# Eight single PSUM banks in one ring in place of one four-bank tile and four single banks

## The chip, the core and the metric

The kernel runs on one core of a Trainium2 chip. TensorE (PE) multiplies and writes its results to PSUM, an accumulator memory of eight banks; one bank holds 512 float32 columns on 128 partitions. VectorE (DVE) and ScalarE (ACT) read PSUM; GpSimd (POOL) does small elementwise work and starts indirect transfers; SyncE (SP) starts the other transfers. The metric is the device time of one execution in microseconds (us). A change counts as faster or slower by its time against the kernel before.

## The reference: what is computed

Two transformer layers over x of shape (8, 256, 128), in float32. Each layer is attention, then a mixture of eight experts, with a layer norm ahead of each and a residual around each:

```python
x = x + _L0_attn_ref(_layernorm(x), ...)   # causal softmax attention, 16 heads of 8, rope, 4 key-value heads
x = x + _L0_ffn_ref(_layernorm(x), ...)    # top-2 of 8 experts, 128 -> 512 -> 128, gelu, plus a shared expert
x = x + _L1_attn_ref(_layernorm(x), ...)   # linear attention in segments of 32, with gated retrieval of past states
x = x + _L1_ffn_ref(_layernorm(x), ...)    # top-2 of 8 experts, 128 -> 512 -> 128, relu
```

In the first attention, with `scale = D ** -0.5`:

```python
scores = jnp.einsum('bqhd,bkhd->bhqk', q, k) * scale
scores = jnp.where(causal[None, None], -jnp.inf, scores)
w = jax.nn.softmax(scores, axis=-1)
out = jnp.einsum('bhqk,bkhd->bqhd', w, v).reshape(b, s, E)
return out @ Wout + bout
```

In the second attention the part that matters here is, for each segment, `A = einsum('bnchk,bndhk->bnhcd', pqc, pkc) * tri`, its product with the values, and a sum over the states of earlier segments weighted by gates.

## The kernel before

The 2048 rows of x stay in SBUF as four batches `xs[b]` of four tiles of 128 rows; a sequence ("row" in the code, class `Row`, L524) is two tiles. There are eight such rows, two to a batch.

**PSUM.** Two pools share the eight banks (L92, L93). `quad()` (L104) gives the one tile `sc` of four banks, for anything that needs four 512-column results at once; `bank()` (L101) gives one of four single banks `mm`. There is one `sc` tile, so whoever wants it next waits until its last reader is done.

**First attention** (`attention0`, L671). For each row, `maxima` (L598) makes the score groups with queries on the partitions and takes their negated maxima; `weighted` (L620) makes them again with keys on the partitions, takes the exponential and multiplies by the values. A score group (`scores`, L580) is four matmuls of 32 rows each (L586), one for each key-value head `j` on the partitions `32j` to `32j+32`, and each writes one bank. Where the tile lies on the diagonal, four more matmuls (L592) add a causal mask of bfloat16, with an identity as weights. Per row there are three groups in `maxima` and three in `weighted`, two of each three masked. One DVE instruction reads all four banks (L608), or one ACT instruction (L637). L640 multiplies by the values into a single bank, DVE copies it out (L648), L651 turns it, L657 and L659 divide, and L663 transposes each half into `oT_bank`, which is held from the start of `weighted`; after the second half `project` (L503) copies and multiplies by the output weights. `maxima` of row r+1 alternates with `weighted` of row r; the preparation of row r+2 (L251, L537 to L576) comes ahead of them. After each second row, `route0` (L690) chooses experts, with a layer norm, `logits` (L301) and small DVE steps.

**Second attention** (`attention1`, L734), by batch. L748 makes four projections of 512 columns, one for each tile, in one `sc` tile; ACT scales the first 256 columns (L752) and the next 128 (L756) of each, DVE copies the last 128 of all four (L761). Then, for each pair of tiles, POOL makes `vm` (L822), PE makes the states (L835, L841, L849), and for each tile k there are four scores of 32 rows (L877), one DVE product with `tri` over the four banks (L881), 16 small matmuls with the values (L891), a copy on ACT (L897), L905, the division (L911 to L914) and a transpose (L917). After `project`, four matmuls (L938) give the states' part, DVE multiplies by the gates, two heads at a time (L946), and sums (L952). The product and POOL's `vm` share one buffer, tagged `vm`.

**Experts** (`experts`, L400): rows are gathered in slots, L431 multiplies by the first weights, ACT or DVE applies the function, L446 multiplies by the second. `dispatch` (L318) finds the slots and sends rows to them by indirect transfers (L368); `chosen` (L475) fetches results the same way (L480).

**Order.** Python generators are woven together: the first attention with the experts of half 0, then the second attention of each batch with the experts of the other half (`weave`, L1007 and L1027 to L1035). A scheduler then fixes one instruction order for each engine by priority and by the buffers that are free; each engine runs its own order strictly and waits on semaphores. `follow(j)` (L108) raises the priority of the matmuls after the first of a group, so that those of a group stand next to each other.

Of the kernel before, what the change touches and what calls it, by code (L numbers as in the profile page):

```python
# [39 lines left out]
P = 128  # L40
B, S, D = 8, 256, 128
NBLK = 4
NT = 4
# [34 lines left out]
def two_layers(  # L78
# [12 lines left out]
    dram = ctx.enter_context(tc.tile_pool(name="slots", bufs=1, space=bass.MemoryType.DRAM))  # L91
    ps4 = ctx.enter_context(tc.tile_pool(name="ps4", bufs=1, space=PSUM))  # L92
    ps1 = ctx.enter_context(tc.tile_pool(name="ps1", bufs=4, space=PSUM))  # L93

    names = iter(range(10**6))

    def tl(pool, shape, tag, dt=FP, bufs=None):
        kw = {} if bufs is None else {"bufs": bufs}
        return pool.tile(shape, dt, tag=tag, name=f"{tag}_{next(names)}", **kw)

    def bank():  # L101
        return tl(ps1, [P, 512], "mm")

    def quad():  # L104

        return tl(ps4, [P, G, 512], "sc")

# [155 lines left out]

    def small(tag, shape=(P, NT, E)):
        return tl(sm, list(shape), tag)

# [51 lines left out]
    def dispatch(half, b1s):  # L318
# [17 lines left out]

        c3, tiles = small("cap3", (P, E, HT)), small("tiles", (P, E))
        nc.vector.tensor_tensor(
            c3, last(pc[:, 0:E], HT), const("cap").rearrange("p (e c) -> p e c", e=E), ALU.is_gt
        )  # L340
        nc.vector.tensor_reduce(tiles, c3, AX.X, ALU.add)
        u3, ends, starts = small("upto3", (P, E, E)), small("ends", (P, E)), small("starts", (P, E))
        nc.vector.tensor_tensor(
# [5 lines left out]

        base, pos = small("base", (P, E)), small("pos", (P, HT, E))  # L350
# [4 lines left out]
        ph, at = small("posk", (P, 2, HT, E)), small("at", (P, 2, HT))  # L355
        nc.vector.tensor_tensor(
# [167 lines left out]
    class Row:  # L524
# [55 lines left out]
        def scores(self, lhsT, rhs, mask):  # L580

            sc = quad()
            for j in range(KVH):
                rows = slice(32 * j, 32 * j + 32)
                with follow(j):
                    nc.tensor.matmul(  # L586
                        sc[:, j, :], lhsT=lhsT[rows], rhs=rhs[rows], start=True, stop=mask is None
                    )
            for j in range(KVH):
                if mask is not None:  # L590
                    with follow(1):
                        nc.tensor.matmul(  # L592
                            sc[:, j, :].rearrange("p (i k) -> p i k", i=G), lhsT=identb, rhs=mask,
                            start=False, stop=True,
                        )
            return sc

        def maxima(self):  # L598

            for qt in range(2):  # L600
                nms = []
                for kt in range(qt + 1):
                    nm = small(f"nmax{kt}", (P, KVH, G))
# [4 lines left out]
                    nc.vector.tensor_reduce(  # L608
                        nm, sc.rearrange("p j (i k) -> p j i k", i=G), AX.X, ALU.max, negate=True
                    )  # L610
                    nms.append(nm)
                    if kt == qt:
                        dst = self.qx[:, qt, :, :, HD].rearrange("p i j -> p j i")
                        if qt:
                            nc.vector.tensor_tensor(dst, *nms, ALU.min)
                        else:
                            nc.vector.tensor_copy(dst, nms[0])
                    yield

        def weighted(self):  # L620
            oT_bank = bank()
            for qt in range(2):
# [9 lines left out]
                for kt in range(qt + 1):  # L632
                    sc = self.scores(
                        self.kxT[:, kt * P : (kt + 1) * P], qm, causTb if kt == qt else None
                    )
                    pT = tl(big, [P, KVH, BT], "at", bufs=2)
                    nc.scalar.activation(pT, sc, AF.Exp)  # L637
                    for j in range(KVH):
                        with follow(j):
                            nc.tensor.matmul(  # L640
                                po[32 * j : 32 * j + 32, :], lhsT=self.vx[:, kt, j, :],
                                rhs=pT[:, j, :], start=(kt == 0), stop=(kt == qt),
                            )
                    if kt < qt:
                        yield
# [4 lines left out]
                for i in range(G):  # L650
# [11 lines left out]
                )  # L662
                nc.tensor.transpose(  # L663
                    oT_bank[:, qt * P : (qt + 1) * P], on.rearrange("p j i d -> p (j i d)"), ident
                )
# [68 lines left out]
    def attention1(x):  # L734
# [12 lines left out]
        for t in range(NT):  # L747
            nc.tensor.matmul(  # L748
                pp[:, t, :], lhsT=xlT[:, t * P : (t + 1) * P], rhs=wqkvu, start=True, stop=True
            )  # L750
        for t in range(NT):
            nc.scalar.activation(  # L752
                s2[:, t].rearrange("p a d -> p (a d)"), pp[:, t, 0 : 2 * D],
                AF.Copy, scale=r[:, t : t + 1],
            )
            nc.scalar.activation(  # L756
                va1[:, t, :, 0:HD],
                pp[:, t, 2 * D : 3 * D].rearrange("p (h c) -> p h c", h=H),
                AF.Copy, scale=r[:, t : t + 1],
            )  # L760
        nc.vector.tensor_copy(u, pp[:, :, 3 * D :])  # L761

# [54 lines left out]
        for b in range(RB):  # L817
# [49 lines left out]

            oT_bank = bank()
            for k in range(2):
# [4 lines left out]
                for j in range(G):  # L874
                    rows = slice(32 * j, 32 * j + 32)
                    with follow(j):
                        nc.tensor.matmul(  # L877
                            sc[:, j, :].rearrange("p (i k) -> p i k", i=G),
                            lhsT=pkT[rows, cols], rhs=pqm[rows, :, cols], start=True, stop=True,
                        )  # L880
                nc.vector.tensor_tensor(  # L881
                    at.rearrange("p j i k -> p (j i) k"),
                    sc.rearrange("p j (i k) -> p (j i) k", i=G),
                    const("tri").unsqueeze(1).to_broadcast([P, H, P]), ALU.mult,
                )

# [17 lines left out]
                for i in range(G):  # L904
# [7 lines left out]
                nc.vector.reciprocal(rec, rec)  # L912
                on = tl(wk, [P, G, G, HD], "on")
# [3 lines left out]
                nc.tensor.transpose(  # L917
                    oT_bank[:, k * P : (k + 1) * P], on.rearrange("p j i d -> p (j i d)"), ident
                )
                yield  # L920
            pw = project(oT_bank, wot_s)
            xo = tl(wk, [P, 2, D], "xo", bufs=1)
            nc.vector.tensor_tensor(xo, pw, xl[:, t0 : t0 + 2, :], ALU.add)

            for k in range(2):
# [9 lines left out]
                for j in range(G):  # L935
                    rows = slice(32 * j, 32 * j + 32)
                    with follow(j):
                        nc.tensor.matmul(  # L938
                            py[:, j, 0 : n_seen * 32].rearrange("p (n i c) -> p n i c", i=G, c=HD),
                            lhsT=pqT[rows, t * P : (t + 1) * P], rhs=st4[rows, 0:n_seen, :, 0:HD],  # L940
                            start=True, stop=True,
                        )
# [177 lines left out]
```

## Time and profile before

| | |
|---|---|
| median of 3 runs | 1099.59 us (1095.2 to 1102.19) |
| profiled execution, its own time | 1101.3 us |
| its span, first to last instruction | 1099.5 us |
| mean granted TensorE clock | 0.697 |
| busy: PE, DVE, ACT, POOL | 655.6, 423.0, 243.8, 211.5 us |
| chain that ended last, by engine | PE 48%, DVE 18%, POOL 10%, ACT 9%, issue 8%, DMA 5% |

The page lists groups of instructions by line: engine, operation, output from input with their shapes, how many, then busy us and mean ns of one, then how long the engine was idle just before them and what ended that idle time. A line of the timeline has the start in us, the length in us, the engine, the line of the code, and in brackets the idle time before it with its cause. A line of the table of stretches has its bounds, then length, busy us and count of PE, of its weight loads (PEld), of DVE, ACT and POOL, then the granted clock (1 is full), the share of DMA time and GB/s. Matmuls in float32 appear as two passes each.

### The profile page before, as it was taken

The numbers are of one execution on the slowest core, as the hardware profiler recorded it, in microseconds if no ns is written. First come the engines' busy times: TensorE is split into PE (matmuls) and PEld (weight loads), VectorE is DVE, ScalarE is ACT, GpSimd is POOL, SyncE is SP. The second block draws the span as 40 slices with busy tenths as digits, with TensorE's granted clock in tenths as the row PEclk, the third lists the DMA queues.
The fourth block names the chain that finished last, engine by engine and source line by source line (L and its number), as shares of the span: only waits on it lengthen the run. The fifth ranks groups of instructions, "written<-read, shape, count | busy, mean of one in ns | idle before, by whom it ended". The sixth has DMA issues, their size and how long they took to land.

```text
span 1099.5 us, 11701 instructions
## 1 busy us (share of the span) xinstructions
PE 655.6 (60%) x4154; PEld 444.6 (40%) x4170; DVE 423.0 (38%) x1121; ACT 243.8 (22%) x505; POOL 211.5 (19%) x267
## 2 busy tenths in 40 slices
PE   3666555655566677775138649873059759730970
PEld 2222221324122454465115427773037647630970
DVE  4422433235131513041246545442247657541431
ACT  1212121201213434431121014341022122200320
POOL 5000100003300000006440220104721120166005
PEclk9856557655565868876665559995559869955995
DMA  7000000001200222314400004743204413214861
GB/s 213 1 0 1 0 1 1 1 1 52 82 0 20 77 58 58 89 53 129 133 14 1 1 0 129 206 117 112 62 6 135 125 46 87 66 48 134 261 207 55
DMA packets 103786, 76.35 MB, mean 69 GB/s; under 512 B 7520, under 2 KB 89776, under 8 KB 103728
## 3 DMA queue, kind: packets, MB, share of 16 engines
q1 hardware_dynamic: 98304, 66.04, 20.8%
q0 software_dynamic: 4096, 8.40, 2.4%
q10 hardware_dynamic: 1328, 1.17, 0.4%
q8 instruction: 33, 0.54, 0.2%
q14 instruction: 25, 0.20, 0.1%
HBM read 61.30 MB, written 14.29 MB: 69 GB/s over the span
## 4 chain that ended last, share of the span: by engine, by line
PE 48%; DVE 18%; POOL 10%; ACT 9%; issue 8%; DMA 5%; another core or an unknown queue 1%; SPq 0%; POOLq 0%; ACTq 0%; DVEq 0%
PE sc L586 7%; PE mm L431 7%; PE mm L446 6%; DVE nmax L608 5%; POOL yt L480 4%; ACT at L637 4%; PE sc L592 3%; PE mm L640 3%; POOL xg L368 3%; PE sc L748 2%; PE sc L877 2%; PE mm L891 2%; DMA w<-in_w 2%; PE mm L497 2%; PE mm L905 1%
## 5 line engine op out<-in xcount | busy, mean ns | idle before, releaser
L441 ACT ACTIVATE hT<-mm,bias 128x128 f32<-128x128 f32 x276 | 84.9, 371 | 234.9 <-PE mm L431 198.1
L446 PE MATMUL mm<-w,hT 128*128 128x128 f32 x736 | 114.1, 295 | 18.4 <-issue 11.8
L431 PE MATMUL mm<-xrT,w 128*128 128x128 f32 x736 | 117.1, 314 | 6.9 <-DVE xrT L415 6.0
L431 PEld LDWEIGHTS mm<-xrT,w 128*128 128x128 f32 x736 | 106.3, 224 | 17.9 <-DVE xrT L415 10.4
L446 PEld LDWEIGHTS mm<-w,hT 128*128 128x128 f32 x736 | 100.8, 206 | 26.0 <-issue 13.7
L608 DVE TENSOR_REDUCE nmax<-sc 128x16 f32<-128x2048 f32 x24 | 55.0, 2291 | 109.4 <-PE sc L586 71.7
L480 POOL DMA_INDIRECT yt<-yg,slots x64 | 62.3, 974 | 102.9 <-DMA yg<-ys 58.9
L368 POOL DMA_INDIRECT xg<-hrows,slots x64 | 66.6, 1040 | 79.1 <-DVE slots L361 60.8
L640 PE MATMUL mm<-at,vx 128*32 128x512 f32 x192 | 37.7, 871 | 48.9 <-ACT at L637 48.9
L637 ACT ACTIVATE at<-sc 128x2048 f32<-128x2048 f32 x24 | 45.1, 1877 | 81.7 <-PE sc L592 69.7
L586 PE MATMUL sc<-qm,kxT 32*128 32x512 f32 x192 | 42.6, 970 | 25.5 <-DVE nmax L608 16.6
L223 POOL TENSOR_SCALAR rsqrt<-mv 128x4 f32<-128x4 f32 (+1 forms) x24 | 6.1, 254 | 256.2 <-DVE mv L233 251.1
L648 DVE COPY os<-mm 128x512 f32<-128x512 f32 x16 | 11.1, 691 | 113.4 <-PE mm L640 102.0
L251 PE MATMUL mm<-ident,xl 128*128 128x128 f32 x16 | 4.1, 404 | 80.9 <-DVE xl L240 80.9
L955 POOL TENSOR_TENSOR x<-x,hr 128x128 f32<-128x128 f32 x16 | 7.4, 465 | 229.8 <-DVE x L928 216.2
L439 DVE TENSOR_SCALAR hT<-mm,bias 128x128 f32<-128x128 f32 x92 | 31.4, 348 | 36.5 <-ACT hT L441 36.2
L586 PE MATMUL sc<-km,qT 32*128 32x512 f32 x192 | 43.0, 982 | 1.7 <-DVE nmax L608 1.7
L881 DVE TENSOR_TENSOR at<-sc,consts 128x2048 f32<-128x2048 f32 x16 | 36.6, 2287 | 13.7 <-PE sc L877 13.6
L415 DVE COPY xrT<-mm 128x512 f32<-128x512 f32 (+1 forms) x24 | 15.9, 664 | 55.1 <-PE mm L413 34.1
L492 PE MATMUL mm<-ident,gates 128*8 128x128 f32 x32 | 8.1, 407 | 48.5 <-DVE gates L967 21.3
L413 PE MATMUL mm<-ident,xr 128*128 128x128 f32 x92 | 17.8, 325 | 30.8 <-DMA xr<-xg 30.8
L251 PEld LDWEIGHTS mm<-ident,xl 128*128 128x128 f32 x16 | 2.6, 180 | 82.0 <-issue 47.5
(214 smaller groups left out, 1081.3 us busy)
## 6 DMA issues: line engine op xcount, KB each, us to landing
w<-in_w SPq DMA_DIRECT2D x184, 256.0 KB
xr<-xg SPq DMA_DIRECT2D x20, 256.0 KB
yg<-ys SPq DMA_DIRECT2D x20, 256.0 KB
xg<-zero SPq DMA_DIRECT2D x10, 256.0 KB
x<-in_x SPq DMA_DIRECT2D x4, 256.0 KB
xg<-hrows,slots POOLq DMA_INDIRECT x64
yt<-yg,slots POOLq DMA_INDIRECT x64
out<-x SPq DMA_DIRECT2D x4, 256.0 KB
```

The lines of the kernel that those rows point to most:

```text
L368: i = nc.gpsimd.indirect_dma_start(out=xg_h[:, :], out_offset=bass.IndirectOffsetOnAxis(ap=half.slots[:, k, t : t + 1], axis=0), in_=half. ...
L431: nc.tensor.matmul(ph[:, c * P : (c + 1) * P], lhsT=w1s[:, c * P : (c + 1) * P], rhs=xrT[:, t * P : (t + 1) * P], start=True, stop=True,)
L439: nc.vector.tensor_scalar(hT[:, c, :], src, bias, 0.0, ALU.add, ALU.max)
L441: nc.scalar.activation(hT[:, c, :], src, func, bias=bias)
L446: nc.tensor.matmul(po[:, t * D : (t + 1) * D], lhsT=hT[:, c, :], rhs=w2s[:, c, :], start=(c == 0), stop=(c == NC - 1),)
L480: nc.gpsimd.indirect_dma_start(out=yt[:, k, t, :], out_offset=None, in_=yg[half.h][:, :], in_offset=bass.IndirectOffsetOnAxis(ap=half.slot ...
L586: nc.tensor.matmul(sc[:, j, :], lhsT=lhsT[rows], rhs=rhs[rows], start=True, stop=mask is None)
L592: nc.tensor.matmul(sc[:, j, :].rearrange("p (i k) -> p i k", i=G), lhsT=identb, rhs=mask, start=False, stop=True,)
L608: nc.vector.tensor_reduce(nm, sc.rearrange("p j (i k) -> p j i k", i=G), AX.X, ALU.max, negate=True)
L637: nc.scalar.activation(pT, sc, AF.Exp)
L640: nc.tensor.matmul(po[32 * j : 32 * j + 32, :], lhsT=self.vx[:, kt, j, :], rhs=pT[:, j, :], start=(kt == 0), stop=(kt == qt),)
L881: nc.vector.tensor_tensor(at.rearrange("p j i k -> p (j i) k"), sc.rearrange("p j (i k) -> p (j i) k", i=G), const("tri").unsqueeze(1).to_ ...
```

## The change

The two PSUM pools become one pool of eight single banks, and `quad()` returns four of them as a list. Every instruction that read four banks becomes four that read one each: the maxima, the exponential, the product with `tri`; the gate product goes from two heads to one head at a time. The copy of `u` moves from one DVE instruction to four on ACT. `oT_bank` is no longer held: the two normalised halves are kept in SBUF (`ons`), and `project` makes both transposes itself. The maxima of the first query tile are written straight to `qx`, without a copy. Four temporaries of `dispatch` get one buffer in place of three.

```diff
-    ps4 = ctx.enter_context(tc.tile_pool(name="ps4", bufs=1, space=PSUM))
-    ps1 = ctx.enter_context(tc.tile_pool(name="ps1", bufs=4, space=PSUM))
+    ps1 = ctx.enter_context(tc.tile_pool(name="ps1", bufs=8, space=PSUM))
...
     def quad():
-        return tl(ps4, [P, G, 512], "sc")
+        return [bank() for _ in range(G)]
...
-        c3, tiles = small("cap3", (P, E, HT)), small("tiles", (P, E))
+        c3, tiles = small("cap3", (P, E, HT), 1), small("tiles", (P, E))
...
-    def project(oT_bank, w):
+    def project(heads, w):
+        pt = bank()
+        for t in range(2):
+            nc.tensor.transpose(pt[:, t * P : (t + 1) * P], heads[t], ident)
         oT = tl(wk, [P, 2 * P], "oT")
-        nc.scalar.copy(oT, oT_bank[:, 0 : 2 * P])
+        nc.scalar.copy(oT, pt[:, 0 : 2 * P])
...
                     nc.tensor.matmul(
-                        sc[:, j, :], lhsT=lhsT[rows], rhs=rhs[rows], start=True, stop=mask is None
+                        sc[j], lhsT=lhsT[rows], rhs=rhs[rows], start=True, stop=mask is None
                     )
...
-                    nc.vector.tensor_reduce(
-                        nm, sc.rearrange("p j (i k) -> p j i k", i=G), AX.X, ALU.max, negate=True
-                    )
...
+                    for j in range(KVH):
+                        nc.vector.tensor_reduce(
+                            nms[kt][:, j, :], sc[j].rearrange("p (i k) -> p i k", i=G), AX.X,
+                            ALU.max, negate=True,
+                        )
...
-                    nc.scalar.activation(pT, sc, AF.Exp)
+                    for j in range(KVH):
+                        nc.scalar.activation(pT[:, j, :], sc[j], AF.Exp)
...
-                nc.tensor.transpose(
-                    oT_bank[:, qt * P : (qt + 1) * P], on.rearrange("p j i d -> p (j i d)"), ident
-                )
+                ons.append(on.rearrange("p j i d -> p (j i d)"))
                 if qt:
-                    pw = project(oT_bank, wout_s)
+                    pw = project(ons, wout_s)
...
-        nc.vector.tensor_copy(u, pp[:, :, 3 * D :])
+            nc.scalar.copy(u[:, t, :], pp[t][:, 3 * D :])
...
-                nc.vector.tensor_tensor(
-                    at.rearrange("p j i k -> p (j i) k"),
-                    sc.rearrange("p j (i k) -> p (j i) k", i=G),
-                    const("tri").unsqueeze(1).to_broadcast([P, H, P]), ALU.mult,
-                )
+                for j in range(G):
+                    nc.vector.tensor_tensor(
+                        at[:, j], sc[j].rearrange("p (i k) -> p i k", i=G),
+                        const("tri").unsqueeze(1).to_broadcast([P, G, P]), ALU.mult,
+                    )
...
-                for a in range(2):
-                    js = slice(2 * a, 2 * a + 2)
+                for j in range(G):
                     nc.vector.tensor_tensor(
-                        pr[:, js, :, 0:n_seen].rearrange("p j w n -> p j n w"),
-                        py[:, js, 0 : n_seen * 32].rearrange("p j (n w) -> p j n w", w=32),
-                        g[:, t, 0:n_seen].unsqueeze(1).unsqueeze(3).to_broadcast([P, 2, n_seen, 32]),
-                        ALU.mult,
+                        pr[:, j, :, 0:n_seen].rearrange("p w n -> p n w"),
+                        py[j][:, 0 : n_seen * 32].rearrange("p (n w) -> p n w", w=32),
+                        g[:, t, 0:n_seen].unsqueeze(2).to_broadcast([P, n_seen, 32]), ALU.mult,
                     )
```

More of the change, by code (lines that the diff above doesn't have):

```diff
@@ L262, in last, with small @@
         return ap.unsqueeze(2).to_broadcast([P, ap.shape[1], n])
-    def small(tag, shape=(P, NT, E)):
-        return tl(sm, list(shape), tag)
+    def small(tag, shape=(P, NT, E), bufs=None):
+        return tl(sm, list(shape), tag, bufs=bufs)
     def softmax(lg, n):
@@ L341, in dispatch @@
         nc.vector.tensor_reduce(tiles, c3, AX.X, ALU.add)
-        u3, ends, starts = small("upto3", (P, E, E)), small("ends", (P, E)), small("starts", (P, E))
+        u3, ends, starts = small("upto3", (P, E, E), 1), small("ends", (P, E)), small("starts", (P, E))
         nc.vector.tensor_tensor(
@@ L348, in dispatch @@
         nc.vector.tensor_tensor(starts, ends, tiles, ALU.subtract)
-        base, pos = small("base", (P, E)), small("pos", (P, HT, E))
+        base, pos = small("base", (P, E)), small("pos", (P, HT, E), 1)
         nc.vector.tensor_scalar_mul(base, starts, float(P))
@@ L354, in dispatch @@
         )
-        ph, at = small("posk", (P, 2, HT, E)), small("at", (P, 2, HT))
+        ph, at = small("posk", (P, 2, HT, E), 1), small("at", (P, 2, HT))
         nc.vector.tensor_tensor(
@@ L592, in scores @@
                         nc.tensor.matmul(
-                            sc[:, j, :].rearrange("p (i k) -> p i k", i=G), lhsT=identb, rhs=mask,
+                            sc[j].rearrange("p (i k) -> p i k", i=G), lhsT=identb, rhs=mask,
                             start=False, stop=True,
@@ L600, in maxima @@
             for qt in range(2):
-                nms = []
+                dst = self.qx[:, qt, :, :, HD].rearrange("p i j -> p j i")
+                nms = [small(f"nmax{k}", (P, KVH, G)) if qt else dst for k in range(qt + 1)]
                 for kt in range(qt + 1):
-                    nm = small(f"nmax{kt}", (P, KVH, G))
                     sc = self.scores(
@@ L607, in maxima @@
                     )
-                    nc.vector.tensor_reduce(
-                        nm, sc.rearrange("p j (i k) -> p j i k", i=G), AX.X, ALU.max, negate=True
-                    )
[L611 to L617, printed above, removed]
+                    for j in range(KVH):
[3 more added lines that the diff above has]
+                        )
+                    if kt == qt and qt:
+                        nc.vector.tensor_tensor(dst, *nms, ALU.min)
                     yield
         def weighted(self):
-            oT_bank = bank()
+            ons = []
             for qt in range(2):
@@ L748, in attention1 @@
             nc.tensor.matmul(
-                pp[:, t, :], lhsT=xlT[:, t * P : (t + 1) * P], rhs=wqkvu, start=True, stop=True
+                pp[t], lhsT=xlT[:, t * P : (t + 1) * P], rhs=wqkvu, start=True, stop=True
             )
@@ L752, in attention1 @@
             nc.scalar.activation(
-                s2[:, t].rearrange("p a d -> p (a d)"), pp[:, t, 0 : 2 * D],
+                s2[:, t].rearrange("p a d -> p (a d)"), pp[t][:, 0 : 2 * D],
                 AF.Copy, scale=r[:, t : t + 1],
@@ L757, in attention1 @@
                 va1[:, t, :, 0:HD],
-                pp[:, t, 2 * D : 3 * D].rearrange("p (h c) -> p h c", h=H),
+                pp[t][:, 2 * D : 3 * D].rearrange("p (h c) -> p h c", h=H),
                 AF.Copy, scale=r[:, t : t + 1],
             )
-        nc.vector.tensor_copy(u, pp[:, :, 3 * D :])
+            nc.scalar.copy(u[:, t, :], pp[t][:, 3 * D :])
         ft = tl(wk, [P, NT, 2, D], "probs1")
@@ L866, in attention1 @@
             yield
-            oT_bank = bank()
+            ons = []
             for k in range(2):
@@ L877, in attention1 @@
                         nc.tensor.matmul(
-                            sc[:, j, :].rearrange("p (i k) -> p i k", i=G),
+                            sc[j].rearrange("p (i k) -> p i k", i=G),
                             lhsT=pkT[rows, cols], rhs=pqm[rows, :, cols], start=True, stop=True,
                         )
-                nc.vector.tensor_tensor(
-                    at.rearrange("p j i k -> p (j i) k"),
-                    sc.rearrange("p j (i k) -> p (j i) k", i=G),
-                    const("tri").unsqueeze(1).to_broadcast([P, H, P]), ALU.mult,
-                )
+                for j in range(G):
[3 more added lines that the diff above has]
+                    )
                 po = bank()
@@ L912, in attention1 @@
                 nc.vector.reciprocal(rec, rec)
-                on = tl(wk, [P, G, G, HD], "on")
+                on = tl(wk, [P, G, G, HD], "on1")
                 nc.vector.tensor_tensor(
@@ L916, in attention1 @@
                 )
-                nc.tensor.transpose(
-                    oT_bank[:, k * P : (k + 1) * P], on.rearrange("p j i d -> p (j i d)"), ident
-                )
+                ons.append(on.rearrange("p j i d -> p (j i d)"))
                 yield
-            pw = project(oT_bank, wot_s)
+            pw = project(ons, wot_s)
             xo = tl(wk, [P, 2, D], "xo", bufs=1)
@@ L938, in attention1 @@
                         nc.tensor.matmul(
-                            py[:, j, 0 : n_seen * 32].rearrange("p (n i c) -> p n i c", i=G, c=HD),
+                            py[j][:, 0 : n_seen * 32].rearrange("p (n i c) -> p n i c", i=G, c=HD),
                             lhsT=pqT[rows, t * P : (t + 1) * P], rhs=st4[rows, 0:n_seen, :, 0:HD],
```

## The prediction

> **What bounds the kernel now.** I read the slices of the page first, to find stages with different limits.
>
> ```profile
> PE   3666555655566677775138649873059759730970
> DVE  4422433235131513041246545442247657541431
> PEclk9856557655565868876665559995559869955995
> ```
>
> Each digit is a tenth, each column 27.5 us. From 25 to 340 us (first attention, alone) no engine is above 7 tenths and the clock is mostly at half: a chain, not a busy engine. From 345 to 470 us expert matmuls are woven in; 545 to 640 us is the second attention alone; 640 to 970 us has experts beside it. The rest is experts alone and gaps at dispatch, which the change does not reach.
>
> The costly groups name the readers of the four-bank tile:
>
> ```profile
> L608 DVE TENSOR_REDUCE nmax<-sc 128x16 f32<-128x2048 f32 x24 | 55.0, 2291 | 109.4 <-PE sc L586 71.7
> L637 ACT ACTIVATE at<-sc 128x2048 f32<-128x2048 f32 x24 | 45.1, 1877 | 81.7 <-PE sc L592 69.7
> L881 DVE TENSOR_TENSOR at<-sc,consts 128x2048 f32<-128x2048 f32 x16 | 36.6, 2287 | 13.7 <-PE sc L877 13.6
> ```
>
> Readers wait for PE and, in the timeline of one row of the first attention, PE waits for readers:
>
> ```profile
> 88.01 2.09 PE L586 MATMUL sc<-qm,kxT 32*128 32x512 f32 x8 [0.68 <-ACT qm L630]
> 92.02 1.88 ACT L637 ACTIVATE at<-sc 128x2048 f32<-128x2048 f32 x1 [2.59 <-PE sc L592]
> 93.95 1.06 PE L640 MATMUL mm<-at,vx 128*32 128x512 f32 x8 [2.03 <-ACT at L637]
> 96.55 1.89 PE L592 MATMUL sc<-causb,identb 128*128 128x512 bf16 x4
> 98.48 2.29 DVE L608 TENSOR_REDUCE nmax<-sc 128x16 f32<-128x2048 f32 x1 [2.71 <-PE sc L592]
> 101.31 0.33 PE L663 MATMUL mm<-ident,on 128*128 128x128 f32 x1 [1.81 <-DVE on L659]
> 113.28 2.09 PE L586 MATMUL sc<-qm,kxT 32*128 32x512 f32 x8 [2.41 <-DVE nmax L608]
> ```
>
> Fill, read, fill, read: three stalls of about 2 us in one row are what a ring of banks can remove. The first line holds the point that decides for me. One such matmul has a median of 1056 ns (the tile's view, 587 at its fastest), yet eight end in 2.09 us: the four row groups run side by side, in two passes. The stretch of a whole row without routing:
>
> ```profile
> 39.80:88.00 48.20, 31.64 (x127) 12.37 (x128) 13.35 (x25) 7.80 (x9) 0.53 (x2) 0.58 0.00 0
> 632.00:745.00 113.00, 84.47 (x732) 69.55 (x732) 53.14 (x143) 38.54 (x115) 11.97 (x16) 0.85 0.38 110
> ```
>
> It takes 48.2 us at a clock of 0.58; beside experts (second line) PE is three quarters busy at 0.85.
>
> **What the Trainium skill says.** "TensorE: Matmul & The Clock Gate", Part 3: matmuls with 32 rows run concurrently if they lie in different row groups, four of them 3.07 times as fast. The trace agrees (1.06 us each, 2.09 for eight, so four times). "TensorEngine Tiling (Array Packing)", Key Properties: a change of tiling mode drains TensorE. The trace shows that as little: after L586 the first mask starts at once (96.55) or 0.33 us late. The clock page again, Part 1: the clock is at half unless a window of about 3.4 us was busy. The clock row and the two durations, 1056 and 587, agree; whether a lone row group counts as busy, neither says. "Perfetto Trace Analysis", Optimizing Scalar/DVE Operations: each instruction has a fixed cost, some 125 ns for DVE on PSUM; here 2291 ns less 2048 columns at the 1.04 ns that 128x512 against 128x2048 gives, about 160.
>
> **The change, part by part**, against the profiled execution (span 1099.5, 1101.3 us with what lies around; the median of the runs is 1099.59, so the same).
>
> *1. More instructions.* 24 maxima of 2291 ns become 96 of 691 (L648's 128x512 from PSUM): +11.3 us. 16 products at L881 become 64 of 691: +7.6. L946 has 962 ns for 448 columns and 501 for 192, so 1.80 a column and 155 fixed: 224 is 0.56, 96 is 0.33; 32 of each is 28.5 against 21.8: +6.7. L761 (2.7) and the copy at L617 go. DVE +22 us of 423. The exponential: 1877 for 2048 columns and 1056 for 1024 (L766) give 645 for 512, 96 against 45.1 us: +16.8; 16 copies of u at most 374 each (L506): +5.9. In the first attention DVE and ACT are busy 28% and 16% of a row, and pieces run while PE fills the next bank, so I price all but the last piece at nothing there.
>
> *2. PE's order in a masked group.* In the old instruction order four scores stand ahead of four masks; in the new one it is score, score, mask, score, mask, score, mask, mask, in all 32 masked groups (a few with the third score and second mask swapped). A mask uses all rows, so only the first two scores still run together: three waves for one. Cold, a wave is 2.0 us and a mask 0.43: 3x2.0+4x0.43 = 7.7 us against 3.7. At full clock 1.07 and 0.22: 4.1 against 1.9. Lower bound of this cost zero, if the scores overlap the masks after all; upper bound three drains of 0.33 more. I take none of either.
>
> *3. The waits that go.* Exponential and maximum of a bank run while PE fills the next. Row by the new order, cold / full clock: first masked group 7.7/4.1; last exponential 0.75 and L640 1.94/1.07: 2.7/1.8; L648 0.85 and L651 1.3/1.0, which now stand ahead of the next group and hold PE: 2.15/1.85; masked group 7.7/4.1; L625 and qm 1.8/1.35; unmasked scores 2.1/1.07, four exponentials in line 2.5 (1.98 before), L640: 6.5/4.6; unmasked maxima scores, masked group, tail: 12.4/7.0; L648, L651, reciprocal and product 0.75, both transposes, copy, projection: 5.1/4.4; masked group 7.7/4.1; next row's preparation 7.2 as now (129.0 to 136.2). Sum **61.0 cold, 40.5 at full clock; now 48.2**. The clock decides. Outside the preparation PE now waits 14.2 us of the row (three times 2.0 for L637, 6.3 for L608, 1.8 for copies); in the new sum 7.7. So I take windows after the first in a dense stretch to be full, a full-clock share of 0.6 (0.16 now): the row is 61.0-0.6x20.5 = 48.7, +0.5.
>
> *4. Routing rows.* Now PE stands from 129.0 to 133.0 while DVE and POOL work on the layernorm. The new order has a masked group there: -4.0, four times: -16.
>
> *5. Rows beside experts* (345 to 470 us, eight masked groups): PE gets 8x2.1 = 17 us more at full clock, and is idle some 40 us of 125 there; bounds 0 and +17, I take +8.
>
> *6. Second attention.* Its groups have no masks. One batch alone, 562 to 625 us:
>
> ```profile
> 578.95 2.09 PE L877 MATMUL sc<-pqm,kT 32*128 32x512 f32 x8 [0.44 <-ACT pqm L520]
> 580.97 1.88 PE L797 MATMUL mm<-um,xlT 128*128 128x8 f32 x8
> 581.11 2.29 DVE L881 TENSOR_TENSOR at<-sc,consts 128x2048 f32<-128x2048 f32 x1 [1.19 <-PE sc L877]
> 602.35 2.09 PE L877 MATMUL sc<-pqm,kT 32*128 32x512 f32 x8 [0.31 <-DVE at L881]
> 605.20 1.92 POOL L822 TENSOR_TENSOR vm<-va1z,consts 128x432 f32<-128x432 f32 x2
> ```
>
> L797 and L835 to L849 lie beside L881 now. In the new order they stand ahead of the scores and L891 follows the scores directly: four products (0.69 first, some 0.6 each after) are bare, about 2.5 us. ACT gains 1.8 us at the start, as it may read the first bank before the fourth is filled (568.3 now, rsqrt ready at 565.0), copies of u included. The first pair's projection then ends 0.5 late. L938 moves behind the projection: scores 1.9, eight products 3.6, sums 1.64, against nothing left there now but a sum: 4.1 late. Those products share the single buffer of vm with L822 on POOL, so POOL, L835 and all of the second pair start 4 us later, and its scores, issued at 602.35 now, wait as well. Worked through, the batch ends near 639 where it ended at 625: +13. Beside experts 12 tiles with a bare wait of 2.0 before L891 (24), less the waits for the tile that go (L877 5.6, L938 4.0): +14; bounds 0 and 3x13; I take +18. The queues of SP and the DMAs carry the same transfers, and no step moves past one; POOL's is named above. The smaller buffers of dispatch serve uses over 200 us apart: nothing.
>
> Sum: 6x0.5 - 16 + 8 + 13 + 18 = **+26: about 1127 us**.
>
> **Rivals.** *Cold*: a lone row group does not count as busy, so split groups stay at half clock. For: the windows around L329 and L497 (258 to 266 us) look full and the clock stays at half. Against: L586 four abreast has always raised it. 6x12.8 - 16 + 8 + 31 = +100: 1201. *Faster*: the clock. With the reads gone PE is dense, it stays at full clock through the row, 40.5 us. 6x(-7.7) - 16, nothing beside experts, half of the second attention's loss: -46, 1055. Its place is the six rows before 340 us; with part 6 whole it decides from a full-clock share of 0.81. Against: every row still has 7 us of preparation and a 2.5 us line of exponentials, and PEclk is 5 or 6 there now. *No serialisation*: masks and lone waves overlap, a row is 61.0-4x3.8 = 45.8 cold, near 43.5 at today's share: 6x(-4.7) - 16 + 16, 1073; against it, a mask needs every row group. *It does not pipeline*: the ring frees banks early, but PE's queue is in order and the scheduler puts L640, L651 and L891 next, behind their readers; that is in the sum already.
>
> **How the numbers follow.** Forecast case 0.5 (1100 to 1160 on its own), cold 0.25 (1180 to 1230), faster by clock or without serialisation 0.25 (1040 to 1085). Leaving a tenth out at each end: 1060 to 1210. 1% either way, about what a measurement of this kernel can tell from no change, is 1089 to 1111: a fifth of the forecast case falls within, a little of it below. Faster 0.28, same 0.12, slower 0.60.
>
> **What would show it.** Right: lone waves of two L586 passes between masks, a masked group of 4 to 8 us; PE's waits for L608 gone and L637's shortened to below 0.8; clock in rows between 0.7 and 0.85; L891 waiting 2 us behind four short products; second attention alone 13 us longer. Wrong: a row far from 49 us, the clock below 0.6 or above 0.9 there, or the stages beside experts moving by more than 30 us.

## The result, and the profile after

The changed kernel takes 1193.68 us (median of 4 runs, 1185.34 to 1196.55) against 1099.45 us before: 1.085 times as long, 95% interval 1.078 to 1.091. Its profiled execution took 1196.55 us, span 1194.8 us. The forecast was 1127 us in a range of 1060 to 1210. The sign and the range held; the size was +27 us where +94 came. An execution more than 1.5% above the fastest of its kernel counts as slow and stays out of the ratios here and below (the medians are of all runs), which matters for e9 (14 slow runs of 20) and e10 (one of four).

The slices of the page, in columns of 29.9 us now:

```profile
PE   3998868886888978975246648884057857731880
DVE  4322342235131322132244443443245555542340
PEclk9995757565565769896665557995559969965895
```

From 30 to 500 us TensorE is now mostly 8 or 9 tenths busy, where it was 5 to 7. Most of its waits are gone; yet the clock row stays mostly at 5 to 7. (The trace has no clock before 81 us here and the page then shows 9; the durations there are those of half clock.) The groups say what TensorE is busy with:

```profile
L588 PE MATMUL mm<-km,qT 32*128 32x512 f32 x192 | 101.6, 937 | 0.0
L588 PE MATMUL mm<-qm,kxT 32*128 32x512 f32 x192 | 85.8, 881 | 9.5 <-ACT qm L629 7.8
...
L637 ACT ACTIVATE at<-mm 128x512 f32<-128x512 f32 x96 | 52.7, 598 | 68.9 <-PE mm L594 55.2
L640 PE MATMUL mm<-at,vx 128*32 128x512 f32 x192 | 58.7, 805 | 5.1 <-ACT at L637 5.0
L889 PE MATMUL mm<-at,va1z 128*32 128x128 f32 x512 | 43.1, 321 | 18.4 <-DVE at L880 18.1
```

The same groups before:

```profile
L640 PE MATMUL mm<-at,vx 128*32 128x512 f32 x192 | 37.7, 871 | 48.9 <-ACT at L637 48.9
L586 PE MATMUL sc<-qm,kxT 32*128 32x512 f32 x192 | 42.6, 970 | 25.5 <-DVE nmax L608 16.6
L586 PE MATMUL sc<-km,qT 32*128 32x512 f32 x192 | 43.0, 982 | 1.7 <-DVE nmax L608 1.7
```

The scores (L588, L586 before) occupy 187.4 us; they occupied 85.6 us (43.0 and 42.6). It is the same 384 passes. L640 hardly waits for the exponential any more (5.1 us, 48.9 before), and L889, L891 before, waits 18.4 us where it waited 1.6. So one stall went and another came, but the large item is the time of the score matmuls themselves. One masked group of a row, TensorE alone:

```profile
107.96 2.08 PE L588 MATMUL mm<-qm,kxT 32*128 32x512 f32 x4 [0.68 <-ACT qm L629]
109.97 0.61 PE L594 MATMUL mm<-causTb,identb 128*128 128x512 bf16 x1
110.51 2.07 PE L588 MATMUL mm<-qm,kxT 32*128 32x512 f32 x2
112.51 0.61 PE L594 MATMUL mm<-causTb,identb 128*128 128x512 bf16 x1
113.05 2.07 PE L588 MATMUL mm<-qm,kxT 32*128 32x512 f32 x2
115.05 1.03 PE L594 MATMUL mm<-causTb,identb 128*128 128x512 bf16 x2
116.01 2.73 PE L640 MATMUL mm<-at,vx 128*32 128x512 f32 x8
```

A score is two passes. The first wave holds two scores (x4), then a mask, then one score alone (x2), a mask, one alone, two masks. Each wave takes 2.07 us whether it holds one score, two or, as before, four: 8.05 us from 107.96 to 116.01, with no gap and no wait. Two rows without routing, in the view of stretches (length; then busy time of PE, PEld, DVE, ACT, POOL; then the granted clock):

```profile
172.80:223.40 50.60, 43.88 (x128) 15.23 (x128) 14.51 (x32) 11.47 (x23) 0.53 (x2) 0.67 0.00 0
299.60:356.50 56.90, 49.14 (x130) 17.23 (x130) 14.42 (x32) 11.14 (x22) 12.56 (x16) 0.59 0.16 49
```

The same two rows before:

```profile
153.80:200.70 46.90, 28.30 (x129) 11.56 (x131) 13.24 (x24) 10.56 (x14) 0.53 (x2) 0.68 0.00 1
274.10:328.30 54.20, 32.19 (x126) 12.66 (x128) 13.25 (x24) 9.09 (x10) 11.59 (x15) 0.59 0.15 46
```

TensorE is now busy 86 to 87% of these rows, where it was busy about 60%, and the clock is no higher. The forecast case had taken a dense stretch to be at full clock after its first window; only its rival "Cold" had this.

### The profile page after: what moved, and what is told of

Read it like the earlier page. It is cut to its first block, busy times and chain, and to the rows that moved or that the text cites. A ratio compares the mean times of both kernels' runs of the same rounds, so it can differ in the third digit from the quotient of the medians.

```text
span 1194.8 us, 11940 instructions
## 1 busy us (share of the span) xinstructions
PE 817.7 (68%) x4170; PEld 488.9 (41%) x4170; DVE 431.9 (36%) x1261; ACT 258.3 (22%) x595; POOL 210.9 (18%) x267
## 4 chain that ended last, share of the span: by engine, by line
PE 59%; DVE 14%; POOL 10%; issue 6%; ACT 5%; DMA 4%; another core or an unknown queue 2%; SPq 0%; POOLq 0%; ACTq 0%; DVEq 0%
PE mm L588 15%; PE mm L430 7%; PE mm L445 6%; PE mm L640 5%; PE mm L594 4%; POOL yt L479 4%; POOL xg L367 3%; PE mm L889 3%; DVE at L880 2%; PE mm L651 2%; PE mm L746 2%; PE mm L875 2%; PE mm L903 2%; PE mm L496 1%
## 5 line engine op out<-in xcount | busy, mean ns | idle before, releaser
L430 PE MATMUL mm<-xrT,w 128*128 128x128 f32 x736 | 119.7, 315 | 15.3 <-DVE xrT L414 14.1
L588 PE MATMUL mm<-km,qT 32*128 32x512 f32 x192 | 101.6, 937 | 0.0
L588 PE MATMUL mm<-qm,kxT 32*128 32x512 f32 x192 | 85.8, 881 | 9.5 <-ACT qm L629 7.8
L611 DVE TENSOR_REDUCE nmax<-mm 128x4 f32<-128x512 f32 x64 | 41.1, 685 | 87.4 <-PE mm L588 60.3
L637 ACT ACTIVATE at<-mm 128x512 f32<-128x512 f32 x96 | 52.7, 598 | 68.9 <-PE mm L594 55.2
L640 PE MATMUL mm<-at,vx 128*32 128x512 f32 x192 | 58.7, 805 | 5.1 <-ACT at L637 5.0
L594 PEld LDWEIGHTS <-identb 128*128 128x128 bf16 x128 | 10.4, 102 | 115.5 <-issue 115.5
L889 PE MATMUL mm<-at,va1z 128*32 128x128 f32 x512 | 43.1, 321 | 18.4 <-DVE at L880 18.1
L648 DVE COPY os<-mm 128x512 f32<-128x512 f32 x16 | 11.1, 692 | 118.7 <-PE mm L640 118.7
L880 DVE TENSOR_TENSOR at<-mm,consts 128x512 f32<-128x512 f32 x64 | 40.2, 682 | 20.7 <-PE mm L875 20.7
L889 PEld LDWEIGHTS mm<-at,va1z 128*32 128x32 f32 x512 | 22.6, 124 | 48.3 <-DVE at L880 45.6
L412 PE MATMUL mm<-ident,xr 128*128 128x128 f32 x92 | 18.7, 332 | 29.6 <-DMA xr<-xg 29.6
```

Of the source, the lines that this page charges most:

```text
L430: nc.tensor.matmul(ph[:, c * P : (c + 1) * P], lhsT=w1s[:, c * P : (c + 1) * P], rhs=xrT[:, t * P : (t + 1) * P], start=True, stop=True,)
L588: nc.tensor.matmul(sc[j], lhsT=lhsT[rows], rhs=rhs[rows], start=True, stop=mask is None)
L594: nc.tensor.matmul(sc[j].rearrange("p (i k) -> p i k", i=G), lhsT=identb, rhs=mask, start=False, stop=True,)
L611: nc.vector.tensor_reduce(nms[kt][:, j, :], sc[j].rearrange("p (i k) -> p i k", i=G), AX.X, ALU.max, negate=True,)
L637: nc.scalar.activation(pT[:, j, :], sc[j], AF.Exp)
L640: nc.tensor.matmul(po[32 * j : 32 * j + 32, :], lhsT=self.vx[:, kt, j, :], rhs=pT[:, j, :], start=(kt == 0), stop=(kt == qt),)
```

## The experiments

The table has every version that computes the whole. The two stage columns are from the profiled execution, in us: up to the second attention's first projections (L748 before), and from there to the end of the span.

| Version | Median us | Ratio to before, 95% | First attention | The rest |
|---|---|---|---|---|
| before | 1099.45 | | 562.6 | 536.9 |
| the change | 1193.68 | 1.078 to 1.091 | 609.5 | 585.3 |
| e1: masks after all scores | 1075.41 | 0.974 to 0.980 | 495.9 | 576.6 |
| e2: before, split order | 1240.58 | 1.123 to 1.134 | 698.5 | 537.0 |
| e4: before, read in pieces | 1088.38 | 0.986 to 0.992 | 538.4 | 547.6 |
| e5: e1, `pr` out of the buffer of `vm` | 1066.03 | 0.966 to 0.972 | 497.5 | 567.8 |
| e6: e1, scores of both tiles first | 1031.40 | 0.934 to 0.940 | 498.2 | 533.5 |
| e7: e5 and e6 | 1025.83 | 0.929 to 0.936 | 496.9 | 528.7 |
| e8: masks first | 1170.31 | 1.057 to 1.069 | 589.6 | 578.8 |
| e9: masks first, scores kept together | 1097.41 | 0.984 to 0.993 | 500.6 | 575.0 |
| e10: e7 and e9 | 1039.37 | 0.946 to 0.962 | 499.1 | 526.4 |

My theory: the split of the masked groups, at half clock, is most of the loss, and the second attention loses separately. A split group is one whose four scores do not stand next to each other in TensorE's order. The rivals: the number of instructions, the ring's order of whole groups, or a stream that warms the clock whatever its order.

### Split order undone alone (e1), and done alone (e2)

e1 is the changed kernel with one dependency added, for order only, that puts every mask behind the group's last score:

```
-                    nc.tensor.matmul(
+                    last = nc.tensor.matmul(
                         sc[j], lhsT=lhsT[rows], rhs=rhs[rows], start=True, stop=mask is None
-                    )
+                    ).ins
...
+                    tc.add_manual_dep(m, last.name, ORDER, reason="after all scores")
```

> The changed kernel, with the order inside a masked group put back to four scores, then four masks; ring of banks and pieces as in the change. Theory (the split of the masked groups, at half clock, is most of the 94 us): 24 masked groups of the first attention alone go from about 8.0 to 3.7 us, 4.0 us each, less what then waits for the last exponential and maximum; with 8 groups beside experts at about 2 us the whole comes to 50 to 100 us less, near 1130 (1095 to 1145), first attention up to the second attention's first work at 550 to 570 us instead of 609, prefix before row 1 near 42 us instead of 52. Rival (number of instructions or the ring's order of whole groups is the cost): less than 20 us gained, 1175 to 1195, and rows stay above 50 us.

e2 is the kernel before, its tile and readers untouched, with the changed order in the masked groups:

```
-            for j in range(KVH):
...
+            steps = "s0 s1 m0 s2 m1 s3 m2 m3" if mask is not None else "s0 s1 s2 s3"
```

> The kernel before, four-bank tile and its readers untouched, with the order inside a masked group made score, score, mask, score, mask, score, mask, mask. Theory (split): each masked group costs 4.0 us more at half clock and 2.1 at full, and here every reader waits for the whole group, so nothing hides it: 24 x 4.0 + 8 x 2.1 = +113 us at most, +70 to +115, near 1195. Rival (masks and lone scores overlap, or the split only matters with pieces): less than +30, below 1130.

e1 gained 118 us, nearly twice what I expected, and is faster than before. All but 9 us of it lie in the first attention (609.5 to 495.9), and the first masked scores of row 0 came at 42.0 us instead of 52.3. e2 lost 139 us against the runs of before beside it (median 1101.12); in the profiled execution all of the loss lies in the first attention (562.6 to 698.5); its rest, which has no masked groups, is unchanged to 0.1 us. The rival that counts instructions is out, as e1 has the same instructions as the change. But both misses point the same way: a split group costs more than the 4 us that I priced. Two rows of e1 show why:

```profile
130.50:167.90 37.40, 29.28 (x126) 11.74 (x128) 14.13 (x32) 11.00 (x23) 0.53 (x2) 0.87 0.00 1
230.00:273.90 43.90, 30.52 (x126) 12.27 (x129) 13.94 (x32) 9.65 (x19) 11.65 (x16) 0.84 0.18 58
```

These are the two rows shown above of the change. In the first, TensorE takes 29.3 us for what took it 43.9, at a clock of 0.87 instead of 0.67. The split costs its own lone waves, and the clock of all that stands around them.

### What warms the clock (e3), and a split group by itself (e11)

e3 is a kernel of its own, with four stages of which each has one of these bodies, 24 times:

```
            if stage == 0:
                go(0, n % 8)
            elif stage == 1:
                for j in range(4):
                    go(j, 4 * (n % 2) + j)
...
```

`go` is one matmul of 512 columns on the rows `32j` to `32j+32` (or all).

> The output is a copy of x, the whole computation is left out; four stages of 32-row, 512-column float32 matmuls, each after at least 10 us without TensorE: 24 in one row group, 24 times four row groups, 24 times two row groups, 24 with all 128 rows. Theory (a lone row group does not count as busy for the clock): the first stage stays at half clock throughout, about 2.1 us a product with the two passes, some 50 us; four abreast go from 2.1 to 1.1 us a wave within 7 us, some 30 us; 128 rows likewise. Two abreast: open, between. Rival (any unbroken stream counts): all four stages fall to about 1.1 us a step after 3.4 to 7 us, each stage some 28 to 33 us.

Its TensorE timeline, one line a stage (start, duration, passes), lone, four abreast, two abreast, all rows:

```profile
7.66 41.30 PE L37 MATMUL bank<-rest,w 32*128 32x512 f32 x48 [7.66 <-DMA w<-in_w]
57.58 23.05 PE L37 MATMUL bank<-rest,w 32*128 32x512 f32 x192 [8.63 <-DVE rest L47]
93.95 41.33 PE L37 MATMUL bank<-rest,w 32*128 32x512 f32 x96 [13.32 <-DVE rest L47]
147.47 22.48 PE L37 MATMUL bank<-rest,w 128*128 128x512 f32 x48 [12.20 <-DVE rest L47]
```

Each stage is 48 passes deep. Lone and two abreast need 41.3 us, 0.86 a pass; four abreast and all rows 23.05 and 22.48. (I had expected some 50 us of the lone stage.) The clock row of that page, 4.27 us a column, rests on records from 62 us on:

```profile
PEclk9999999999999999999955555555555555589999
```

It is at half through the whole third stage, 41 us without a gap, and rises some 3 us into the fourth. The lone stage lies ahead of the records; that it was at half too is read from its duration, the same as that of two abreast. So a stream on 32 rows, or on 64, did not raise the clock in 41 us. The Trainium skill, "TensorE: Matmul & The Clock Gate", Part 1, says that the clock rises after a sustained busy stretch of about 3.4 us, whatever number of matmuls fills it. For 128 rows and for four row groups this agrees (about 3.3 and 4.4 us here); for one and two row groups the measurement says otherwise, and it decides.

e11 has the masked groups by themselves, between two pauses and without:

```
    for n in range(N):
        group(TOGETHER, n % 2)
    for n in range(N):
        group(SPLIT, n % 2)
```

> The output is a copy of x, the whole computation is left out; only masked groups without readers: 12 in the changed kernel's order after a pause, another pause, then 12 with four scores and four masks, and directly behind them, with no pause, 12 in the changed order again. Theory (the split order cannot hold the full clock, so it pays the half-clock price however dense it is): 7.7 to 8.1 us a group in the first stretch, 12 groups 92 to 97 us; the second stretch starts at 3.8 and is at about 2.0 us a group within 7 us, some 28 us; the third begins at 4.1 us a group and falls back to about 8 within two groups, 85 to 95 us. Rival (a dense stream holds the clock whatever its order): first stretch at 4.1 us a group after 7 us, some 55 us, and the third 49 us.

From its TensorE timeline, the second stretch (together) and the first lines of the third (split, directly behind it):

```profile
112.57 2.09 PE L48 MATMUL bank<-rest,w 32*128 32x512 f32 x8 [9.00 <-DVE rest L62]
114.59 1.82 PE L52 MATMUL bank<-mb,wb 128*128 128x512 bf16 x4
116.33 1.14 PE L48 MATMUL bank<-rest,w 32*128 32x512 f32 x8
...
138.78 1.13 PE L48 MATMUL bank<-rest,w 32*128 32x512 f32 x4
...
143.12 1.73 PE L48 MATMUL bank<-rest,w 32*128 32x512 f32 x4
...
145.32 2.07 PE L48 MATMUL bank<-rest,w 32*128 32x512 f32 x2
```

Together, the first group takes 3.76 us (112.57 to 116.33) and the next eleven 2.04 each (116.33 to 138.78). Split, the first takes 4.3 us (138.78 to 143.12), the clock falls within 5 us, and from the third on each takes 8.05 us, as all of the first stretch did. The rival that a dense stream holds the clock falls. What in the split order loses it, the lone waves themselves or the more frequent change between scores and masks, this run does not separate; e3 shows only that lone waves without masks do not raise it. A split group is thus not 2.1 times as long as an unsplit one, as I had it at either clock, but 8.05 against 2.04 us: a stream of split groups loses the full clock, at which the first of them took 4.3 us.

### Masks first (e8), and the scores kept together (e9, e10)

If only a mask between scores costs, masks could stand in front. In e8 the mask opens the accumulation and the score ends it:

```
+                            sc[j].rearrange("p (i k) -> p i k", i=G), lhsT=identb, rhs=mask,
+                            start=True, stop=False,
...
+                        sc[j], lhsT=lhsT[rows], rhs=rhs[rows], start=mask is None, stop=True
```

> Single banks, but the four masks ahead of the four scores (the masks open the accumulation, the scores end it), second attention as changed. Theory (what costs is a mask between scores; where the masks stand otherwise matters little): scores run four abreast as with masks last, 1060 to 1085; a masked group shortens by at most 4 x 0.22 to 4 x 0.43 us where the masks run before the scores' operands are there, and loses up to three masks' overlap with the first readers. Rival (any mask next to scores breaks them): above 1150.

It took 1170 us, as if the rival were right. But the timeline shows another split, in each masked group of the maxima:

```profile
172.85 2.08 PE L597 MATMUL mm<-km,qT 32*128 32x512 f32 x6
174.86 1.50 PE L655 MATMUL mm<-consts,os 128*128 128x36 f32 x6
176.29 2.07 PE L597 MATMUL mm<-km,qT 32*128 32x512 f32 x2
```

Three scores, then three matmuls of another step, then the last score alone: the first score of a group has no raised priority (`follow(0)`), and once the masks stood in front the scheduler let others pass it. e9 gives it the same priority:

```
-                with follow(j):
+                with follow(j if mask is None else 1):
```

> Masks ahead of the scores as before, but the first score of a masked group has the same priority as the other three, so that nothing stands between them; all else as in the run with masks first. Theory (one score torn from the other three in the 16 masked groups of the maxima cost that run its 95 us, by a lone wave of 2.1 us each and the clock lost with it): back to 1060 to 1090. Rival (masks ahead of scores cost by themselves): above 1130.

The first attention fell from 589.6 to 500.6 us in the profiled execution, which took 1077.36. The first row, from one first masked group of `weighted` to the next, was 47.5 us long in e8 at a clock of 0.64 and is 34.8 in e9 at 0.97:

```profile
47.70:95.20 47.50, 36.00 (x129) 13.52 (x129) 13.77 (x32) 9.79 (x21) 0.53 (x2) 0.64 0.00 1
45.50:80.30 34.80, 24.85 (x128) 9.53 (x128) 13.61 (x32) 9.78 (x21) 0.53 (x2) 0.97 0.00 1
```

The median of 1097.41 us is above the expected range: the 20 runs spread from 1076 to 1110 us, and the mean granted clock with them, from 0.768 down to 0.732; why it varies so here is open. The six runs behind the ratio took 1076 to 1090 us, as expected. The cause named for e8 is confirmed by one priority: two lone waves a row, some 4 us, cost 12.7 us of the row.

> Masks ahead of scores, scores kept together, own buffer for pr, scores of both tiles first. If masks may run before the scores' operands are there, a masked group ends up to 4 x 0.22 us earlier at full clock, less the overlap of the later masks with the first readers: 1010 to 1030, against 1026 with masks last. Rival (the first reader's later start takes all of that back): 1026 to 1040.

e10 shows no gain from the masks' place: 1027.29 us in its profiled execution, 1039.37 in the median, where e7 had 1027.34 and 1025.83. That is where its rival had put it.

### Pieces alone (e4)

The kernel before with its four-bank tile, but L608, L637, L881 and L946 each read it in four pieces:

```
-                    nc.scalar.activation(pT, sc, AF.Exp)
+                    for j in range(KVH):
+                        nc.scalar.activation(pT[:, j, :], sc[:, j, :], AF.Exp)
```

> The kernel before, with its four-bank tile, but the maximum, the exponential, the causal product and the expert products read it in four pieces. Theory (pieces alone are cheap, the ring's order is the cost of the second attention): first attention: 12 groups of exponentials and 12 of maxima bare, (645x4-1877) = 0.7 and (691x4-2291) = 0.5 us each at most, 2 x 12 x 0.6 = +14; second attention +2 to +8; in all +5 to +25, near 1115. Rival (the number of instructions is what costs in the second attention): its lone batch alone +10 or more and the stages beside experts +20 or more, 1140 or above.

Both theories missed: the first attention became 24.2 us shorter, the second 10.7 us longer. L640 may start behind the first piece of the exponential, and the next steps follow; the first row took 38.4 us at a clock of 0.87 instead of 48.2 at 0.58. (TensorE's order changed in many places of the second attention, so the 10.7 us are not the extra instructions alone.)

### The second attention: one buffer (e5), the order (e6), both (e7)

The batch alone takes 92.3 us in e1, 97.4 in the change, with the same order on TensorE, and 83.7 before. From e1's timeline of all engines:

```profile
517.55 1.08 PE L905 MATMUL mm<-consts,rope 128*128 128x36 f32 x8 [0.68 <-ACT rope L897]
518.56 1.14 PE L877 MATMUL mm<-pqm,kT 32*128 32x512 f32 x8
...
519.72 2.48 DVE L882 TENSOR_TENSOR at<-mm,consts 128x512 f32<-128x512 f32 x4 [0.26 <-PE mm L877]
520.46 1.83 PE L891 MATMUL mm<-at,va1z 128*32 128x128 f32 x6 [0.76 <-DVE at L882]
...
537.83 0.59 PE L835 MATMUL mm<-vm,probs 128*32 128x108 f32 x8 [5.38 <-POOL vm L822]
```

The second tile's scores (518.56) come only behind the first tile's last step (L905), and its value products are drawn out behind the DVE products. Before, these scores ran at 585.84, beside the first tile's copy. And at 537.83 the second pair waits for `vm` on POOL. e5 takes the shared buffer away (`pr` goes to the buffer tagged `bias4`, which is not quite its own: the bias of the experts, L392, uses it too), e6 the series: the loop over the two tiles is cut in two, scores and DVE products for both, then the rest.

```
-                pr = tl(wk, [P, G, 32, NST], "vm", bufs=1)
+                pr = tl(wk, [P, G, 32, NST], "bias4", bufs=1)
```

```
+            ons, ats = [], []
+            for k in range(2):
...
+                ats.append(at)
+            for k in range(2):
...
+                at = ats[k]
```

> Single banks, scores then masks, and in addition the products of the states (pr) in a buffer of their own instead of the one they share with POOL's vm. Theory of the prediction's step 6 (after the projection, four products and a sum hold that buffer, so POOL, L835 and the second pair start late): in the batch alone TensorE's 5.4 us before the second pair's L835 go, the batch of 92.3 us becomes about 87, and the three later batches gain 2 to 5 us each: 10 to 20 us less than with the shared buffer, 1055 to 1065. Rival (the loss of the second attention lies in the order of scores and products, not in this buffer): less than 6 us gained, about 1072.

> Single banks, scores then masks, and in the second attention the scores and causal products of both tiles of a pair ahead of the value products of the first; pr still shares its buffer. Theory (the ring put score, product and value product of the two tiles in series): each pair saves a score group of 1.1 to 2.1 us, a bare product of 0.7 and the stretched value products (3.7 instead of 1.9 us), about 4.5 us; the batch alone 92.3 to about 84, six pairs beside experts 0 to 4.5 each: 15 to 30 us less, 1045 to 1060. Rival (the shared buffer is the cost): less than 6 us gained, as the second pair still waits for POOL.

> Both edits together: own buffer for pr and scores of both tiles first. If the two costs are separate, the gains add: 25 to 50 us less than single banks with scores then masks, 1025 to 1050, and the time from the second attention's first projections to the end (576 us with neither, 537 before) comes to 530 to 550. If both stand for one wait, it is no better than the better of the two.

The rest of the span fell by 8.8 us in e5, 43.1 in e6 and 47.9 in e7, to 528.7, below the 536.9 of before. In e5 the batch alone became only 1.3 us shorter, not 5: most of the gain lies in the later batches. e6 gained more than the 15 to 30 us expected. The batch alone took 77.2 us in it, and its second pair went to full clock behind eight scores back to back (16 passes):

```profile
535.59 3.79 PE L876 MATMUL mm<-pqm,kT 32*128 32x512 f32 x16
539.31 2.02 PE L894 MATMUL mm<-at,va1z 128*32 128x128 f32 x32
542.06 1.08 PE L908 MATMUL mm<-consts,rope 128*128 128x36 f32 x8 [0.73 <-ACT rope L900]
```

L908 (L905 in e1) takes 1.08 us here, 1.92 in e1; that the scores raised the clock fits e3, but was not tried by itself. Of the two, the order counts for most and the buffer for little. But e6 does not restore the order of before, it makes a better one (77.2 us against 83.7), so its 43.1 us are not a measure of what the ring's order had cost. e7, at 1025.83 us, is 0.932 times the time before and 168 us below the change.

## Why the prediction was right in direction and wrong in size

The loss of the profiled execution, 95.3 us, is 46.9 in the first attention and 48.4 in the rest. The experiments cut the first into parts: pieces -24.2 (e4), the ring with the smaller edits of the change -42.5 (e4 to e1), the split +113.6 (e1 to the change; in the kernel before, e2, it cost +135.9). The rest: pieces +10.7, the ring +29.0, and 8.7 that the change has over e1 with the same order on TensorE. Of these 5.1 lie in the batch alone, whose first 35.5 us have a clock of 0.60 in the change and 0.74 in e1; why the clock differs is open, and the four runs of the change lie 11 us apart.

**Step 1, instructions.** The durations were right (685 ns for 691, 598 for 645, 682 for 691), but the busy time added on DVE was 8.9 us, not 22: pieces in line overlap a little (four products in 2.48 us at L882 of e1), and the sum had them end to end. That pieces hide was right, that they gain by themselves was not seen.

**Step 2, the split.** Order and price held: 8.05 us at half clock for 7.7, 4.3 at full clock (e11) for 4.1. The lower bound, overlap of scores and masks, is excluded by the timelines.

**Step 3, the clock share of 0.6, is the step that failed.** It rested on the sentence that a dense stretch is full clock after the first window. The rows shown have clocks of 0.67 and 0.59, which are shares of 0.34 and 0.18, because a stream of split groups does not keep the full clock (e11: 8.05 us a group instead of 2.04). With these shares, my own sum of 61.0 less 20.5 times the share gives 54.0 and 57.3; measured were 50.6 and 56.9. The first is 3.4 us off, and the second agrees in part by luck: that row took 54.2 us before, 6 us more than the row of the sum. So the sum was usable and the share was not. I had the "Cold" rival with this mechanism and gave it 0.25, with the argument that four scores abreast had always raised the clock: so it is in an unbroken stream (e3), but in the first attention the change leaves only the unmasked score groups four abreast. Three rows without routing took 13.9 us more in all, where 1.5 was forecast.

**Left out: row 0's preparation.** Its three maxima groups, two of them split at half clock, hold TensorE ahead of the next row's preparation, and the first masked group of `weighted` starts 12.5 us later (39.8 to 52.3). No term had it; e1 brings it back to 42.0.

**Step 4**, the wait of -4 us in a routing row filled by a masked group: the two routing intervals before 340 us took 1.8 us more in all, not 7 less. The group that fills the wait is itself 6.7 and 8.0 us long there.

**Step 5**, with the last rows: 18.7 us more from 328 us to the second attention, where the sum has +8 for the experts' stage and -8 for the two later routing waits; just outside the bound of 17, which was counted at full clock.

**Step 6.** The batch alone: +13.7, forecast 13, in part by luck: e1, with the same order on TensorE, has +8.6. Beside experts +34.7, forecast 18, within the bound of 39. I had credited 9.6 us for waits that go. Both mechanisms were there, but their order of size was not as forecast: the series score, product, value product was the larger part, the shared buffer the small one (e6, e5).

**Rivals.** "Cold", at 1201 us, is the case whose mechanism came. That its total lies so near is luck: it has +69 us in the first attention and +31 in the second, measured were 46.9 and 48.4. "Faster" needed the full clock, which no split order kept; the rows of e1, without the split, come near it and take 37 and 44 us. "No serialisation" is excluded by e11. "It does not pipeline" was so for L889 and for L651, which waits 11.8 us behind L648 where it waited 1.6, and not for L640.

## What to carry to other kernels

Keep matmuls of 32 rows that can run abreast next to each other in TensorE's order. Here a mask between two scores made them pay the wave again (2.07 us each), and the lower clock made what stands around them pay too. A busy TensorE in the profile is no sign of a fast one: the change's row was 87% busy at a clock of 0.67 and took 50.6 us, e1's 78% at 0.87 and took 37.4. Look at how many of its row groups are abreast, and at the clock beside it. When a buffer is cut into smaller ones, compare the instruction order of each engine first; here two orders held back more than the ring and the pieces gained, and each was mended in a few lines.

## What had not been expected of the hardware

A row group alone, or two abreast, without a gap for 41 us, left the clock at half; four abreast raised it in about 4.4 us. A stream of split masked groups that began at full clock lost it within 5 us although TensorE had no gap, and a group went from 4.3 us to 8.05, where a group with its scores together took 2.04.
